# Block products on thirds (15 for 18) in place of halves (7 for 8) for the projections of a two-layer graph-attention kernel

## The chip, the cores and the metric

The kernel runs on one core of a Trainium2 chip. TensorE is the engine of the matrix products (matmuls); their results land in the banks of PSUM, from which ScalarE or VectorE read them (0.37 and 0.42 us for 128x256 in the trace of the kernel before). Tokens and weights lie in SBUF, the memory on the chip. GpSimd is a third engine for elementwise work, and transfers from and to the main memory (DMA) are issued by SyncE (SPq in the lines below). The time is the device time of one execution in microseconds (us); lower is better.

## The reference

128 graphs of 64 nodes with 768 features are normalised, sent through two attention layers and added to the input. All is fp32.

```python
h = jnp.maximum(_layernorm(x, axis=-1), 0.0)
for l in range(2):
    m_left  = einsum('bsh,oh->bso', h, W_left[l])
    m_right = einsum('bsh,oh->bso', h, W_right[l])
    u_left  = einsum('bih,bjh->bij', h, m_left) / temper        # u_right likewise
    u = u_left * adj_tri + u_left * diag_mask + u_right * swapaxes(adj_tri, 1, 2)
    delta_exp_u = exp(u) * adj
    attention = delta_exp_u / (sum(delta_exp_u, axis=2, keepdims=True) + 1e-10)
    h_lin = einsum('bsh,oh->bso', h, W_lin[l]) + b_lin[l]
    h = relu(layer_norm(attention @ h_lin, ln_a[l], ln_b[l]))
out = x + h
```

Nearly all the work is three 768x768 projections per layer: left, right and linear.

## The kernel before

Tokens go in 16 groups of 512. Each layer has a pass one (left and right projections, scores, softmax) and a pass two (linear projection, attention times it, layer norm). A projection is split in halves of inputs, outputs and tokens, and done as 7 block products instead of 8. The products run in PSUM banks X, Y, Z, V; a product that adds to an earlier one is chained in the same bank after it has been read.

```python
ORDER = (("X", "A11", "B11"), ("Y", "S2", "T2"), ("Z", "S1", "T1"), ("V", "S3", "T3"),
         ("X", "A12", "B21"), ("Z", "S4", "B22"), ("V", "A22", "T4"))

def project(u, k, g, between=None):            # once per side k and per 128 output columns g
    for i, (at, a, t) in enumerate(ORDER):
        ...                                    # a fresh bank at the first product in it
        for c in range(CH):                    # CH = 3
            nc.tensor.matmul(p, w[a][:, c, g * P:(g + 1) * P], b[t][:, c, :], ...)   # width 256
        ...                                    # one read of the bank per product (ScalarE or VectorE)
        pump(1)                                # one piece of side work from a queue
```

M, the projected tokens, lies in the long-lived pool `big`. The side work (normalising and transposing the next tokens, relu of loaded tokens, softmax steps, sums of tokens on GpSimd) comes from one queue, a piece per product.

Of the kernel before, what the change touches and what calls it, by code (L numbers as in the profile page):

```python
# [17 lines left out]
def kernel(  # L18
# [24 lines left out]

# [5 lines left out]
    CH = C // 2  # L49
    HH = H // 2  # L50
    PAIR = P // S
    Q = 4
# [3 lines left out]
    assert L == 2 and PAIR == 2 and C == 6 and HH <= 512  # L56
# [16 lines left out]
    queue = deque()  # L73
# [3 lines left out]
    def pump(n):  # L77
        for _ in range(n):
            f = queue.popleft() if queue else None
            if f is None and idle:  # L80
                f = idle.popleft()
            if f is not None:
                f()

    def flush():
        while queue:
            pump(1)


    SRC = {"l": w_left, "r": w_right, "n": w_lin}  # L90
    W = {}

    def load_w(l, kind):
        v = SRC[kind][l].rearrange("(c p) o -> p c o", p=P)
        t = {}
        for s in ("A11", "A21", "A22", "A12", "S1", "S2", "S4"):
            t[s] = wpool.tile([P, CH, HH], F32, name=f"w_{kind}_{s}")
        for s in ("A11", "A21", "A22", "A12"):
            i, o = int(s[2]) - 1, int(s[1]) - 1
            nc.sync.dma_start(t[s], v[:, i * CH:(i + 1) * CH, o * HH:(o + 1) * HH])  # L100
        W[l, kind] = t

    def centre(l):

        t = W[l, "n"]
        for a, b in (("A11", "A21"), ("A12", "A22")):
            m = stat.tile([P, 2, CH], F32, name="wm", bufs=2)
            idle.extend(none * 2)

            def means(a=a, b=b, m=m):  # L110
                nc.vector.reduce_sum(m[:, 0], t[a], axis=mybir.AxisListType.X)
                nc.vector.reduce_sum(m[:, 1], t[b], axis=mybir.AxisListType.X)
                nc.vector.tensor_add(m[:, 0], m[:, 0], m[:, 1])
                nc.vector.tensor_scalar_mul(m[:, 0], m[:, 0], 1.0 / H)

            idle.append(means)
            for s in (a, b):
                idle.extend(none * 2)
                idle.append(lambda s=s, m=m: nc.gpsimd.tensor_sub(
                    t[s], t[s], m[:, 0].unsqueeze(2).to_broadcast([P, CH, HH])))  # L120

    def sums_w(l, kind, eng, to, apart=0):
        t = W[l, kind]
        t["S3"] = t["A21"]
        for o, f, a, b in (("S1", "tensor_add", "S3", "A22"), ("S2", "tensor_sub", "S1", "A11"),
                           ("S3", "tensor_sub", "A11", "S3"), ("S4", "tensor_sub", "A12", "S2")):
            to.extend(none * apart)
            to.append(lambda o=o, f=f, a=a, b=b: getattr(eng, f)(t[o], t[a], t[b]))


    ORDER = (("X", "A11", "B11"), ("Y", "S2", "T2"), ("Z", "S1", "T1"), ("V", "S3", "T3"),
             ("X", "A12", "B21"), ("Z", "S4", "B22"), ("V", "A22", "T4"))
# [4 lines left out]
    def tokens_of(key):  # L137
        ht = HT[key]
        r = {f"B{i + 1}{t + 1}": ht[:, i * CH:(i + 1) * CH, t * TH:(t + 1) * TH]
             for i in range(2) for t in range(2)}  # L140
        r.update(TS.get(key, {}))
        return r

    def sums_t(key, eng=nc.gpsimd):

        ts = TS[key] = {}

        def sub(o, m, n):
            ts[o] = big.tile([P, CH, TH], F32, name="ts", bufs=6)
            b = tokens_of(key)  # L150
            eng.tensor_sub(b[o], b[m], b[n])  # L151

        for o, m, n in (("T1", "B12", "B11"), ("T2", "B22", "T1"), ("T3", "B22", "B12"), ("T4", "B21", "T2")):
            queue.append(lambda o=o, m=m, n=n: sub(o, m, n))
# [58 lines left out]
    def affine(which, l, u, step=1):  # L213
# [6 lines left out]
        for c in range(0, C if l else 0, step):  # L220
            queue.append(lambda c=c: part(c))

    def transpose_rows(l, u, pool):

        key, xr = (1, l, u), XR[l, u]
        if l == 0:
# [16 lines left out]
            if u:  # L243
                queue.extend(stats + [lambda: scale(0, Q)] + norms)
            else:
                scales = [lambda q=q: scale(q, q + 1) for q in range(Q)]
                queue.append(stats[0])
                for q in range(Q):
                    queue.extend(stats[q + 1:q + 2] + [scales[q], norms[q]])
        if (l, u) == (0, 0):  # L250
# [12 lines left out]
            for c in range(0, C, 2):  # L263
                queue.append(lambda c=c: turn(c))
            queue.append(lambda: nc.sync.dma_start(KEPT[l][u], ht))
            return
# [9 lines left out]
        for q in range(Q):  # L276
            queue.append(lambda q=q: nc.vector.transpose(
                xb[:, :, q, :], xr[q].rearrange("p (b j) -> p b j", j=32)))
        queue.append(store)


    def pass_one(l, aside):
        with tc.tile_pool(name=f"one{l}", bufs=2, reuse_waits="tile") as sp:
            ADJ, WM, CHAIN = {}, {}, {}
# [6 lines left out]
            def masks(u):  # L291

                WM[u] = sp.tile([P, Q, 2, S], F32, name="wm")
                for k in range(2):
                    t = tri[:, k].unsqueeze(1).to_broadcast([P, Q, S])
                    nc.gpsimd.tensor_tensor(WM[u][:, :, k], ADJ[u][:, :, 1 - k], t, op=ALU.mult)

            def softmax(u):
                return [lambda: next(CHAIN[u], None)] * 6

            def prepare(u):

                transpose_rows(l, u, sp)
                queue.append(lambda: load_h(1, l, u))
                if u + 1 < NB:
                    queue.append(lambda: load_rows(l, u + 1, sp))
                queue.extend(softmax(u - 2) if u > 1 else [])
                queue.append(lambda: load_adj(u))
                queue.extend(none * (6 if u > 1 else 9))
                affine(1, l, u)  # L310
                sums_t((1, l, u))

            M = {}

            def project(u, k, g, between=None):

                b, w = tokens_of((1, l, u)), W[l, "lr"[k]]
                bank = {}
                for i, (at, a, t) in enumerate(ORDER):
                    new = at not in bank  # L320
                    if new:
                        bank[at] = ps_st.tile([P, 512], F32, name=at)
                    p = bank[at][:, :TH]
                    for c in range(CH):
                        nc.tensor.matmul(p, w[a][:, c, g * P:(g + 1) * P], b[t][:, c, :],  # L325
                                         start=(new and c == 0), stop=(c == CH - 1),
                                         skip_group_check=True)
                    if i == 2 and k == 0 and g == 0:
                        M[u] = [big.tile([P, CH, T // S, 2, S], F32, name="n") for _ in range(2)]
                    if i >= 3:  # L330
                        half, first = ((1, 4), (0, 0), (0, 4), (1, 0))[i - 3]
                        to = M[u][half][:, g, first:first + 4, k, :]
                        pb = p.rearrange("p (b s) -> p b s", s=S)
                    if i == 0:
                        s1 = sp.tile([P, TH], F32, name="s1", bufs=1)
                        nc.scalar.copy(s1, p)  # L336
                    elif i == 1:
                        u2 = sp.tile([P, TH], F32, name="u2", bufs=1)
                        nc.vector.tensor_add(u2, p, s1)  # L339
                    elif i == 2:  # L340
                        u4 = sp.tile([P, TH], F32, name="u4", bufs=1)
                        nc.vector.tensor_add(u4, p, u2)  # L342
                    elif i == 4:
                        nc.scalar.copy(to, pb)  # L344
                    else:
                        nc.vector.tensor_add(to, pb, (u4 if i == 3 else u2).rearrange("p (b s) -> p b s", s=S))  # L346
                    if i == 1 and between:
                        between()
                    pump(1)

            def scores(u):

                ht, m = HT[1, l, u], M[u]
                p = ps_aux.tile([P, 2, T], F32, name="aux")[:, 0].rearrange("p (q m) -> p q m", q=Q)
                for q in range(Q):
                    for c in range(C):
                        for h in range(PAIR):
                            b = q * PAIR + h
                            nc.tensor.matmul(p[h * S:(h + 1) * S, q, :], ht[:, c, b * S:(b + 1) * S],  # L359
                                             m[c // CH][:, c % CH, b].rearrange("p k j -> p (k j)"),  # L360
                                             start=(c == 0), stop=(c == C - 1))
                wm, adj = WM[u], ADJ[u]

                def chain():
                    um = sp.tile([P, Q, 2, S], F32, name="um", bufs=1)
                    nc.vector.tensor_tensor(um.rearrange("p q k j -> p (q k j)"), p.rearrange("p q m -> p (q m)"),
                                            wm.rearrange("p q k j -> p (q k j)"), op=ALU.mult)
                    yield
                    v = sp.tile([P, Q, S], F32, name="v", bufs=1)
                    nc.vector.tensor_add(v, um[:, :, 0], um[:, :, 1])  # L370
# [12 lines left out]
                    at = sp.tile([P, 2, Q, 32], F32, name="at", bufs=1)  # L383
# [8 lines left out]

            if l == 0:
# [5 lines left out]
                transpose_rows(0, 0, sp)  # L399
# [289 lines left out]
```

## Time and profile before

| | before |
|---|---|
| time, median (lowest to highest of 4 runs) | 2944.11 us (2943.38 to 2945.45) |
| TensorE busy, instructions | 99%, 14872 |
| mean granted TensorE clock | 0.997 |
| VectorE, ScalarE, GpSimd busy | 38%, 20%, 26% |
| first product of the first group to first product of the second | 18.39 to 73.96 us = 55.57 us |

TensorE is the bound, and it stands for some 27 us in all: 12.5 us for ScalarE in the transposes at the very beginning, 11.8 us once in the middle, and about 2 us of small waits. The line of the 11.8 us is quoted in the prediction; that of the first is `PE aux L257 <- ACT x L239: 12.5, 4, 9.0` (us in total, times, longest). In the timeline the columns are start, duration, engine, source line, operation, output<-inputs, shapes, records; a bracket gives the idle time before and what ended it.

```profile
18.39 1.64 PE L325 MATMUL X<-ht,w_l_A 128*128 128x256 f32 x6
20.76 1.56 PE L325 MATMUL Y<-ts,w_l_S 128*128 128x256 f32 x6 [0.73 <-DVE ts L151]
```

The first product of this kernel uses raw weights and raw tokens, so it starts as soon as the tokens are transposed; only the second waits, 0.73 us, for a sum. A group of later tokens takes 59.98 us, of which 5.6 us are scores of the group before; without scores its own work is 54.4 us. The first group took 55.57 us. This kernel's start is nearly free of waits.

### The profile page before, as it was taken

To read this page: it belongs to the slowest core of one execution; us is meant where nothing else is said; L and a number is where in the kernel's file an instruction comes from. 1 tells how busy PE (TensorE), PEld (TensorE's weight loads), DVE (VectorE), ACT (ScalarE), POOL (GpSimd) and SP (SyncE) were. 2 spreads that over 40 slices of the span, in tenths; PEclk is the share of its full clock that TensorE was granted. 3 is DMA by queue.
4 is the path that set the end of the run, shared out by engine and by line. 5 is a ranking of instruction groups with operands and counts; after the bars stand their busy time and mean duration, and the time that the engine had idled before them with its cause. 6 is when DMAs were issued, how large, how long until landed. Compare 5 with 4: busy or idle time off the path is not lost.

```text
span 2942.2 us, 37469 instructions
## 1 busy us (share of the span) xinstructions
PE 2901.8 (99%) x14872; PEld 2241.3 (76%) x14872; DVE 1125.1 (38%) x2316; ACT 583.1 (20%) x1113; POOL 754.9 (26%) x478
## 2 busy tenths in 40 slices
PE   8999999999999999999998999999999999999998
PEld 7888888888888655555587888888888886555554
DVE  5444333433343232222333333333333324555555
ACT  2121112111120122222311111111111112232321
POOL 0321111111111262322312211111111114556564
PEclk9999999999999999999999999999999999999999
DMA  6424422342232343332454422343223304555544
GB/s 188 120 71 109 101 71 70 91 114 75 71 77 66 104 151 105 101 122 92 140 126 108 114 75 70 79 112 90 70 71 96 93 24 117 175 154 153 179 142 132
DMA packets 228656, 310.24 MB, mean 105 GB/s; under 512 B 53632, under 2 KB 179072, under 8 KB 220288
## 3 DMA queue, kind: packets, MB, share of 16 engines
q1 hardware_dynamic: 228192, 307.05, 37.6%
q8 instruction: 117, 1.92, 0.3%
q10 hardware_dynamic: 288, 0.79, 0.1%
q14 instruction: 59, 0.48, 0.1%
HBM read 202.91 MB, written 104.86 MB: 105 GB/s over the span
## 4 chain that ended last, share of the span: by engine, by line
PE 97%; DMA 1%; DVE 1%; SPq 0%; issue 0%; ACT 0%; POOL 0%; DVEq 0%; POOLq 0%
PE Z L325 17%; PE V L325 17%; PE X L325 17%; PE Y L325 8%; PE Z L567 8%; PE V L567 8%; PE X L567 8%; PE aux L359 6%; PE Y L567 5%; PE aux L495 3%; DMA x<-z 0%; DMA w_n_A<-in_w_lin_dram 0%; DMA h<-xb 0%; DMA at<-att 0%; PE aux L257 0%
## 5 line engine op out<-in xcount | busy, mean ns | idle before, releaser
L151 POOL TENSOR_TENSOR ts<-ht 128x768 f32<-128x768 f32 x126 | 241.0, 1913 | 1532.3 <-DMA ht<-h 579.5
L325 PE MATMUL V<-ts,w_l_A 128*128 128x256 f32 x1152 | 281.4, 380 | 11.8 <-DVE n L346 11.8
L325 PE MATMUL X<-ht,w_l_A 128*128 128x256 f32 x1152 | 280.2, 379 | 0.0
L325 PE MATMUL X<-ht,w_r_A 128*128 128x256 f32 x1152 | 280.2, 379 | 0.0
L325 PE MATMUL V<-ts,w_r_A 128*128 128x256 f32 x1152 | 280.0, 379 | 0.0
L567 PE MATMUL X<-w_n_A,ht 128*128 128x384 f32 x768 | 268.8, 486 | 0.0
L567 PE MATMUL V<-w_n_A,ts 128*128 128x384 f32 x768 | 268.6, 486 | 0.0
L344 ACT COPY n<-X 128x256 f32<-128x256 f32 x192 | 71.5, 372 | 968.8 <-PE X L325 968.8
L346 DVE TENSOR_TENSOR n<-V,u 128x256 f32<-128x256 f32 x384 | 161.9, 422 | 237.0 <-PE V L325 236.4
L325 PEld LDWEIGHTS V<-ts,w_l_A 128*128 128x128 f32 x1152 | 219.6, 191 | 42.1 <-DVE n L346 12.2
L151 POOL TENSOR_TENSOR ts<-ht,ts 128x768 f32<-128x768 f32 x126 | 238.8, 1895 | 40.6 <-issue 38.5
L325 PEld LDWEIGHTS X<-ht,w_l_A 128*128 128x128 f32 x1152 | 219.0, 190 | 30.3 <-issue 0.6
L325 PEld LDWEIGHTS X<-ht,w_r_A 128*128 128x128 f32 x1152 | 219.2, 190 | 29.9
L325 PEld LDWEIGHTS V<-ts,w_r_A 128*128 128x128 f32 x1152 | 218.9, 190 | 29.8
L567 PEld LDWEIGHTS V<-w_n_A,ts 128*128 128x128 f32 x768 | 145.9, 190 | 101.8
L567 PEld LDWEIGHTS X<-w_n_A,ht 128*128 128x128 f32 x768 | 145.8, 190 | 101.6 <-issue 0.3
L521 ACT ACTIVATE z<-aux 128x768 f32<-128x768 f32 x128 | 102.6, 807 | 596.5 <-PE aux L495 582.5
L339 DVE TENSOR_TENSOR u<-Y,s 128x256 f32<-128x256 f32 x192 | 81.5, 424 | 356.4 <-PE Y L325 349.4
L346 DVE TENSOR_TENSOR n<-Z,u 128x256 f32<-128x256 f32 x192 | 81.4, 424 | 304.2 <-PE Z L325 304.1
L342 DVE TENSOR_TENSOR u<-Z,u 128x256 f32<-128x256 f32 x192 | 81.5, 424 | 282.3 <-PE Z L325 282.1
L336 ACT COPY s<-X 128x256 f32<-128x256 f32 x192 | 71.2, 371 | 583.9 <-PE X L325 583.9
L577 POOL TENSOR_TENSOR u2b<-u,b 128x384 f32<-128x384 f32 x64 | 63.9, 999 | 474.1 <-DVE u L575 443.4
(107 smaller groups left out, 3959.4 us busy)
## 6 DMA issues: line engine op xcount, KB each, us to landing
ht<-h SPq DMA_DIRECT2D x63, 1536.0 KB, 7.0
h<-xb SPq DMA_DIRECT2D x124, 384.0 KB, 6.1
z<-z SPq DMA_DIRECT2D x128, 192.0 KB, 2.9
x<-z SPq DMA_DIRECT2D x128, 192.0 KB, 8.6
xr<-in_x_dram SPq DMA_DIRECT2D x128, 192.0 KB, 3.4
out_dram<-xr SPq DMA_DIRECT2D x128, 192.0 KB, 2.7
x<-in_x_dram SPq DMA_DIRECT2D x120, 192.0 KB, 8.3
adj<-in_adj_dram SPq DMA_DIRECT2D x64, 128.0 KB, 2.8
```

Of the source, the lines that this page charges most:

```text
L151: eng.tensor_sub(b[o], b[m], b[n])
L325: nc.tensor.matmul(p, w[a][:, c, g * P:(g + 1) * P], b[t][:, c, :], start=(new and c == 0), stop=(c == CH - 1), skip_group_check=True)
L336: nc.scalar.copy(s1, p)
L339: nc.vector.tensor_add(u2, p, s1)
L342: nc.vector.tensor_add(u4, p, u2)
L344: nc.scalar.copy(to, pb)
L346: nc.vector.tensor_add(to, pb, (u4 if i == 3 else u2).rearrange("p (b s) -> p b s", s=S))
L359: nc.tensor.matmul(p[h * S:(h + 1) * S, q, :], ht[:, c, b * S:(b + 1) * S], m[c // CH][:, c % CH, b].rearrange("p k j -> p (k j)"), start= ...
L495: nc.tensor.matmul(cx[k][i, m, :HH], at[j, q, :], hl[j, q, m * HH:(m + 1) * HH], start=True, stop=True)
L521: nc.scalar.activation(zs[k].rearrange(two, n=2), cx[k], AF.Square, accum_out=ss[:, k:k + 1])
L567: nc.tensor.matmul(p, b[t][:, c, r * P:(r + 1) * P], w[a][:, c, :], start=(new and c == 0), stop=(c == CH - 1), skip_group_check=True)
L577: nc.gpsimd.tensor_add(u2b, u2, rows["b2"])
```

## The change

The intent: fewer TensorE passes. Inputs and outputs are split in thirds of 256 features and tokens in halves: 18 block products, which a bilinear scheme does with 15. A block product is now 2 inner x 2 outer matmuls of width 256. In the linear projection that is 60 matmuls of width 256 per group instead of 42 of width 384, so fewer columns pass through TensorE although its instructions rise. All 15 are read from PSUM over 128x512, and banks are chained more tightly: X takes products 0, 2, 4, 6, 8, 10. In pass two the bias is copied into the fresh banks by ScalarE instead of being added afterwards. The queue gives way to numbered slots, two per product.

```diff
-    ORDER = (("X", "A11", "B11"), ("Y", "S2", "T2"), ...)                    # 7
+    ORDER = ((8, "X", "ta", "+2"), (5, "Z", "u1", "-0+2"), (0, "X", "u2", "+3"), (1, "Y", "u3", "-3"),
+             (12, "X", "B3", "-5"), (6, "V", "B0", "-2"), (2, "X", "td", "-4"), (4, "Y", "tb", "+1"),
+             (10, "X", "B4", "+0-2"), (7, "V", "B1", "+3"), (3, "X", "u0", "+1-3"), (11, "Y", "te", "+0"),
+             (13, "V", "tc", "-1"), (9, "Z", "tg", "+4"), (14, "V", "tf", "+5"))  # weight, bank, tokens, where it goes
+    W_SUMS = (...)   # 17 sums of 128x512 per weight matrix instead of 4 of 128x1152
+    T_SUMS = (...)   # 11 sums of 128x512 per group of tokens instead of 4 of 128x768

+    def read(p, to, i, seen):                 # first use of an output: ScalarE copies; later: VectorE adds
+        ...
+                nc.scalar.activation(to(o), p, AF.Copy, scale=1.0 if sign == "+" else -1.0)
+        ...
+                added(nc.vector, to(o), sign, to(o), p)

     def project(...):
-                    M[u] = [big.tile([P, CH, T // S, 2, S], F32, name="n") for _ in range(2)]
+                    M[u] = sp.tile([P, C, NBB, 2, S], F32, name="m", bufs=1)      # sp: the pool of this pass
...
     # start of layer 0
-                        sums_w(0, "r", nc.vector, queue, 1)
+                        rs = sums_w(0, "r", nc.gpsimd)
+                        for n in range(0, len(rs), 3):
+                            put(10 + n // 3, *rs[n:n + 3])
...
     def linear(...):                          # pass two, two blocks of 128 tokens together
+                    nc.scalar.copy(b, BIAS[:, PRELOAD[i]].unsqueeze(1).to_broadcast([P, len(rs), D]))
-                        nc.vector.tensor_add(s1, p, rows["b1"])
...
```

## The prediction

> **What bounds the kernel now.** I read the page from the top: busy shares, the slices, the chain that ended last, and then the groups with their shapes.

> ```profile
> span 2942.2 us, 37469 instructions
> PE 2901.8 (99%) x14872; PEld 2241.3 (76%) x14872; DVE 1125.1 (38%) x2316; ACT 583.1 (20%) x1113; POOL 754.9 (26%) x478
> ...
> PEclk9999999999999999999999999999999999999999
> ...
> PE 97%; DMA 1%; DVE 1%; SPq 0%; issue 0%; ACT 0%; POOL 0%; DVEq 0%; POOLq 0%
> ```

> The reader is to see that TensorE is the bound, at full clock, and that every other engine is below 40%. Only two things can move the time: fewer TensorE passes, or new TensorE idleness. So I need the pass time and the waits, from the timeline of TensorE.

> ```profile
> 434.97 1.46 PE L325 MATMUL X<-ht,w_l_A 128*128 128x256 f32 x6
> 436.26 1.46 PE L325 MATMUL Y<-ts,w_l_S 128*128 128x256 f32 x6
> 437.65 5.46 PE L359 MATMUL aux<-n,ht 128*64 128x128 f32 x96
> ...
> 1231.19 2.10 PE L567 MATMUL X<-w_n_A,ht 128*128 128x384 f32 x6
> 1233.13 2.10 PE L567 MATMUL Z<-w_n_S,ht 128*128 128x384 f32 x6
> ```

> A product is 3 matmuls and leaves 6 records, two per fp32 matmul. From start to start a product of width 256 takes 1.295 us, so 0.4317 us a matmul; one of width 384 takes 1.935 us, so 0.645 us. The mean of one record in the groups (380 ns, 486 ns) is longer than the step, because records overlap; it must not be multiplied by counts. The scores block takes 5.4 us and 0.2 us of change-over.

> The one long TensorE stall of this kernel is in the waits: V of L325 waited 11.8 us, once.

> ```profile
> PE V L325 <- DVE n L346: 11.8, 1, 11.8
> ...
> DVE wm L111 <- DMA w_n_A<-in_w_lin_dram: 11.6, 1, 11.6
> ```

> At 1552 us of the span VectorE stood in its queue at a sum over weights that had not landed, with a PSUM read behind it.

> [...] A record here is half an fp32 matmul, 215.8 ns from start to start[...]. [...] the trace has 681 ns for the 128x512 product with a PSUM operand (L366). [...] the trace has 1283 ns in all 31 of them.

> **The change part by part.**

> 1. *Projections of the tokens (left, right).* Before: 2 sides x 3 output columns x 7 products x 3 matmuls = 126 matmuls of width 256 per group of 512 tokens. After: 2 x 15 products x 2 x 2 = 120, same width and weight shape. There are 16 groups x 2 layers: 192 matmuls fewer x 0.4317 = **-83 us**. "15 for 18" sounds like a sixth, but the old form already had 7 for 8, so it is 1/21.

> 2. *The linear projection.* Before: 42 matmuls of width 384 per group, 27.09 us. After: 60 of width 256, 25.90 us. Difference 1.19 x 32 = **-38 us**. More weight loads, but the left/right stage already runs loads at this rate with TensorE at its step.

> 3. *Reads of PSUM.* They get twice as wide: 18 reads of 128x512 per 15 products, 6 on ScalarE (590 ns, the copy from PSUM at L260) and 12 on VectorE (681 ns). Per project 8.2 us of VectorE in 25.9 us: throughput is no question. Latency is. Bank X is used at products 0, 2, 4, 6, 8, 10 with a single product between. A product lasts 4 x 0.4317 = 1.727 us; the record of the last matmul ends 0.16 us after its step, VectorE starts 0.04 us later (in the timeline), TensorE restarts 0.05 us after a read. Left for the reads: 1.727 - 0.25 = 1.47 us. One read on ScalarE fits. Product 8 has two VectorE reads: 2 x 0.681 + 0.04 = 1.40 us plus some 0.1 us for a weight load that can't be taken ahead: zero to 0.13 us of wait, in 64 projects and 32 linears. I take 0.07 x 96 = **+7 us**.

> 4. *What stands ahead of those reads.* This I followed in the order of instructions of the changed kernel. In layer 0, ahead of the read of product 4 on ScalarE, stand the table load (1.28), the square root (0.3, then 0.4 for VectorE's reciprocal and bias) and three normalisations of 128x768 (1.02 each, L239). Count from the end of product 0: scores to 5.5, product 1 to 7.2, product 2 to 8.95, its read to 9.75, table and root to 11.3, first normalisation from 11.75, third done at 14.6, read of product 4 done at 15.2. Product 6 could start at 14.1: about 1.1 us of wait. At product 14 the softmax on VectorE (with a table load for Exp) delays the read of product 12 by some 0.3 us. Together 1.4 x 15 groups = **+20 us**. In layer 1 there are no normalisations, and the softmax lies before product 8: nothing.

> 5. *Start, borders, end.* The first sums of weights and tokens (31 instead of 8 for the left side) run on VectorE ahead of products 0 to 14: start 2.3 us later and some 4 us of waits: **+6 us**. At the border from pass one to pass two, product 0 now needs a bias preload on ScalarE, queued behind the last softmax's Exp, some 3.5 us after the scores; before, TensorE went straight on: 2 x 3.5 = **+7 us**. The last group of each linear stage runs in products of half the size (0.86 us) with only 0.6 us for reads: **+6 us** for two. Its last context waits for the previous one's buffers: 2 x 3 = **+6 us**.

> 6. *The stall of 11.8 us.* The sums over weights now come some 12 free slots later, after the weights have landed: **-12 us**.

> 7. *GpSimd.* 11 token sums of 128x512 (1.3 us, estimated from 1.9 us for 128x768) instead of 4: 14 us per group instead of 7.6, in 57 or 29 us. They are done well before product 6 of the next group: off the path. The bias adds of pass two on GpSimd go.

> Sum: -83 - 38 - 12 + 7 + 20 + 6 + 7 + 6 + 6 = -81. 2944.6 - 81 = **2864 us**, 2.7% faster.

> **The rivals.**

> *The bare count of passes.* If the reads always hide, only 1, 2 and 6 remain with a few us at the borders: about 2820 us. For it: the wider reads are below half the throughput of both engines. Against: with one product between two uses of X, and in-order queues, any normalisation or softmax step ahead of a read becomes TensorE idleness, which the old order (X again after 4 products, 5.2 us) could absorb.

> *The banks become the bound.* If the two-read gap at product 8 costs 0.4 us rather than 0.07 (a read slowed by the strided output, or VectorE late), that is 96 x 0.33 = 32 us more: 2896 us, within 2%. For it: my slack there is zero. Against: the strided reads of 128x256 took 422 ns now[...], and even beside a busy GpSimd they don't spread. VectorE's steps with two SBUF inputs do: the last add of pass two (L534) takes 1.41 us on the mean, 0.95 us alone.

> *The last pass overloads VectorE or the transfers.* There VectorE has 12 reads, 4 scaled products (1.0 us) and 4 last adds (up to 1.7 us), about 19 of 29 us per group, and TensorE's slots must wait for ScalarE's relu of tokens still being loaded (7 us per load, 155 GB/s in this stage). One or two us per group would add 15 to 30 us: 2880 to 2895 us. Against: I followed the queue and found read 12 done at 5.05 us where product 14 starts at 5.18.

> **Range and chances.** The gains (133 us) rest on counts and a step measured to a per mille; I trust them to 3 us. The losses (52 us) are sums of small waits that could be 20 or 110. Hence 2836 to 2894. Faster by over 2% means below 2885.7 us: losses below 74 us. I give that 0.80; within 2% 0.19; slower would need 190 us of waits, against which the other engines' shares speak: 0.01.

> **What would show it right or wrong.** The step of width 256 should still be 1.295 us per 6 records, with 7680 records in the left/right stage and 3840 in the linear. A group of the left/right stage should take 57.4 us in layer 1 and about 58.8 in layer 0 (60.0 now); a pair of linears 29.2 to 29.4 us (30.4 now). Waits of TensorE for ScalarE should stand at X in layer 0, those for VectorE at X after product 8 with under 0.15 us each. The 11.8 us wait should be gone. Wrong would be: GpSimd named as TensorE's releaser, waits at X in layer 1, or a linear pair over 30 us.

What is left of the cut paragraph are times measured in the kernel before; its last clause means ScalarE's 31 table loads of 1283 ns. That a product chained into a bank waits for the read of the one before, on which steps 3 and 4 rest, is seen there in V's wait of 11.8 us: the product starts at 1565.25 us, 0.05 us after VectorE's read of V (0.42 us from 1564.78 us). The 0.1 us for a weight load in step 3 is the difference between 1.56 us for a product whose first load starts with it (at 443.04 us) and 1.46 us for one whose load starts 0.21 us earlier (at 436.26 us). The strided reads of 128x256 that "don't spread" take 0.43 us at most, alone as beside GpSimd; the last add of pass two takes 0.95 us in all 29 cases alone and up to 2.54 us beside it.

## The result and the profile after

The output is correct. The changed kernel took 2898.03 us (median of 4 runs, 2894.96 to 2902.79) against 2944.11: the ratio is 0.9844, 95% interval 0.9827 to 0.9861. Ratios here are the mean time of one kernel's runs over that of the other's runs of the same rounds, so not quite the ratio of the medians. The gain is 1.6%, where 2.7% was predicted, and 2898.03 lies 4 us above the predicted range.

The head of the page of the changed kernel, with its slices of granted clock and its chain of what ended last:

```profile
span 2896.5 us, 39904 instructions
PE 2804.7 (97%) x15640; PEld 2387.1 (82%) x15640; DVE 1307.7 (45%) x2126; ACT 842.5 (29%) x1453; POOL 1195.0 (41%) x934
...
PEclk8999999999999999999999999999999999999998
...
PE 83%; DMA 6%; DVE 4%; ACT 4%; SPq 1%; issue 1%; POOL 0%; ACTq 0%; DVEq 0%; POOLq 0%
```

TensorE's share fell from 99% to 97% and its part in the chain from 97% to 83%: more of that chain is now work of others that TensorE waits for. The first and the last slice of the clock are at 8 tenths; the mean clock is 0.989, where it was 0.997. The waits of TensorE in the changed kernel (engine, bank, line, what it waited for: us in total, times, longest):

```profile
PE X L354 <- ACT m L189: 31.8, 22, 7.3
PE aux L293 <- ACT x L275: 12.3, 4, 8.9
PE X L601 <- ACT hl L189: 8.2, 3, 5.5
PE X L354 <- DVE w_l L144: 7.8, 2, 5.7
PE Y L354 <- DVE w_l L144: 5.4, 1, 5.4
PE X L601 <- ACT X L584: 4.8, 2, 2.4
```

The 11.8 us stall is gone, and the 12.3 us of the beginning stand in both kernels. The rest is new. The steady state is what the prediction said. Second group of layer 0, the timeline of TensorE:

```profile
105.12 1.89 PE L354 MATMUL X<-ht,w_l 128*128 128x256 f32 x8
106.85 1.89 PE L354 MATMUL V<-ht,w_l 128*128 128x256 f32 x8
109.80 1.97 PE L354 MATMUL X<-ts,w_l 128*128 128x256 f32 x8 [1.06 <-ACT m L189]
```

A product starts 1.73 us after the one before, 4 x 0.432 us as before the change. Product 6, in X, waits 1.06 us for ScalarE's read of product 4, in 14 groups: the wait of step 4, at the place named there. From scores to scores a group of layer 0 takes 58.68 us (59.98 before), the best groups of layer 1 57.39 us, and a pair of linears 29.20 us. The excess is elsewhere, in places that come once or twice each.

**The beginning.** Timeline of the changed kernel, GpSimd, VectorE and TensorE:

```profile
14.73 27.25 POOL L144 TENSOR_TENSOR w_r<-w_r,w_r 128x512 f32<-128x512 f32 x17 [12.98 <-DMA w_r<-in_w_right_dram]
...
19.04 5.08 DVE L144 TENSOR_TENSOR w_l<-w_l,w_l 128x512 f32<-128x512 f32 x3
...
24.18 3.78 PE L354 MATMUL X<-ts,w_l 128*128 128x256 f32 x8 [5.71 <-DVE w_l L144]
...
37.42 0.67 DVE L144 TENSOR_TENSOR m<-m,Z 128x512 f32<-128x512 f32 x1
37.56 3.78 PE L354 MATMUL Y<-ts,w_l 128*128 128x256 f32 x8 [5.36 <-DVE w_l L144]
...
49.25 2.74 DVE L144 TENSOR_TENSOR w_l<-w_l,w_l 128x512 f32<-128x512 f32 x4
```

Three left-weight sums take VectorE 5.08 us while GpSimd sums the right weights, some 1.67 us each from start to start; four take 2.74 us once GpSimd has finished at 42.0 us, 0.60 us from start to start, or 0.72 us where a sum reads the result of the one before. The add at 37.42, which has one operand in PSUM, takes its usual 0.67 us even beside GpSimd. The products that follow these waits of 5.71 and 5.36 us last 3.78 us instead of 1.89. The second group starts at 92.63 us instead of 73.96. Less each kernel's own work (51.8 us and 54.4 us), that is 40.8 us against 19.6: the beginning costs 21 us more.

**The first group of layer 1.** Timeline of the changed kernel:

```profile
1464.79 0.60 ACT L189 ACTIVATE m<-X 128x512 f32<-128x512 f32 x1 [4.40 <-DMA z<-z]
...
1465.53 3.75 PE L354 MATMUL X<-ts,w_l 128*128 128x256 f32 x8 [7.32 <-ACT m L189]
```

ScalarE's first read of X waits for a store of `z`, rows of the pass before. M has moved from `big` into the pool of the pass, whose memory those rows still held. In the same group:

```profile
1495.15 0.34 SPq L248 DMA_DIRECT2D ht<-h  x1
...
1502.10 1.52 ACT L255 ACTIVATE ht<-ht,b_col,a_col 128x512 f32<-128x512 f32 x2 [7.67 <-DMA ht<-h]
1503.52 0.57 ACT L189 ACTIVATE m<-X 128x512 f32<-128x512 f32 x1
...
1504.15 3.57 PE L354 MATMUL X<-ht,w_r 128*128 128x256 f32 x8 [6.91 <-ACT m L189]
```

Here ScalarE stands at the relu of tokens whose load has been issued at 1495.15, and the read of X is behind it in its queue. X is named with `m` and ScalarE, but the true releaser is the transfer, which landed at 1502. The product starts 0.06 us after the read ends (1503.52 + 0.57). Further groups of layer 1 show the same wait with 0.2 to 1.25 us. Their mean over 14 groups is 57.74 us, 0.35 us over the best; in the control run below it is only 0.10 us over it, so this part differs from run to run. In the first linear of layer 1 it comes a third time, 5.47 us before the product at 2419.60.

**The borders.** The two waits of 2.4 us for the bias copy in X (L584), where pass one turns into pass two.

### The profile page after: what moved, and what is told of

Its sections match the earlier page's. It is cut to its first block, busy times and chain, and to the rows that moved or that the text cites. A ratio compares the mean times of both kernels' runs of the same rounds, so it can differ in the third digit from the quotient of the medians.

```text
span 2896.5 us, 39904 instructions
## 1 busy us (share of the span) xinstructions
PE 2804.7 (97%) x15640; PEld 2387.1 (82%) x15640; DVE 1307.7 (45%) x2126; ACT 842.5 (29%) x1453; POOL 1195.0 (41%) x934
## 4 chain that ended last, share of the span: by engine, by line
PE 83%; DMA 6%; DVE 4%; ACT 4%; SPq 1%; issue 1%; POOL 0%; ACTq 0%; DVEq 0%; POOLq 0%
PE X L354 18%; PE V L354 12%; PE X L601 11%; PE Y L354 9%; PE V L601 8%; PE Z L354 6%; PE aux L376 6%; PE Y L601 5%; PE Z L601 4%; PE aux L520 3%; DMA ht<-h 2%; DMA h<-xb 2%; ACT ht L255 1%; DVE st L220 1%; ACT x L275 1%
## 5 line engine op out<-in xcount | busy, mean ns | idle before, releaser
L144 POOL TENSOR_TENSOR ts<-ht 128x512 f32<-128x512 f32 x441 | 585.8, 1337 | 1227.2 <-DMA ht<-h 519.5
L144 POOL TENSOR_TENSOR ts<-ht,ts 128x512 f32<-128x512 f32 x189 | 249.3, 1324 | 200.7 <-PE X L354 99.6
L354 PE MATMUL X<-ts,w_l 128*128 128x256 f32 x1024 | 246.8, 384 | 27.8 <-ACT m L189 22.1
L601 PE MATMUL X<-w_n,ts 128*128 128x256 f32 x1024 | 246.0, 382 | 6.6 <-ACT X L584 4.8
L354 PE MATMUL X<-ts,w_r 128*128 128x256 f32 x1024 | 242.9, 380 | 2.9 <-ACT m L189 2.8
L354 PEld LDWEIGHTS X<-ts,w_l 128*128 128x128 f32 x1024 | 193.0, 192 | 63.1 <-issue 28.3
L601 PEld LDWEIGHTS X<-w_n,ts 128*128 128x128 f32 x1024 | 193.0, 191 | 38.4 <-issue 5.8
L354 PEld LDWEIGHTS X<-ts,w_r 128*128 128x128 f32 x1024 | 191.4, 190 | 34.9 <-ACT m L189 6.1
L354 PE MATMUL Y<-ts,w_l 128*128 128x256 f32 x768 | 183.7, 382 | 5.4 <-DVE w_l L144 5.4
L601 PE MATMUL Y<-w_n,ts 128*128 128x256 f32 x768 | 182.4, 379 | 0.0
L354 PE MATMUL Y<-ts,w_r 128*128 128x256 f32 x768 | 181.4, 379 | 0.0
L354 PEld LDWEIGHTS Y<-ts,w_l 128*128 128x128 f32 x768 | 147.4, 192 | 26.2 <-DVE w_l L144 5.8
L354 PEld LDWEIGHTS Y<-ts,w_r 128*128 128x128 f32 x768 | 145.9, 190 | 19.8
```

The lines of the kernel that those rows point to most:

```text
L144: (eng.tensor_add if sign == "+" else eng.tensor_sub)(o, a, b)
L354: nc.tensor.matmul(p[:, g], w[ORDER[i][0]][:, c, g * P:(g + 1) * P], b()[t][:, c, :], start=(new and g == c == 0), stop=(c == K2 - 1), ski ...
L601: nc.tensor.matmul(p[:, n], b[t][:, c, r * P:(r + 1) * P], w[s][:, c, :], start=(i in FIRST and i not in PRELOAD and n == c == 0), stop=(c ...
```

## The experiments

The control and e1 to e3 ran on one chip together, e4 to e7 on another, each with 9 runs of the kernel before (median 2942.56 and 2943.4 us). A gain over the control is given as the difference of the two ratios times 2943 us; since each ratio has an interval of about 0.0013 to either side, such a gain is known to some 5 us, and where it is smaller the trace has to decide.

**c_after**, the changed kernel, unaltered, as control.

> The changed kernel again, unaltered, on the chip and in the rounds of the three that follow: a control. All theories: 2898 us within 0.2%, ratio to before 0.984 to 0.986. In the profile the first product of the second group (X at the left side) starts at 92 to 93 us, layer 0 has 14 waits of 1.06 us at X, and layer 1 begins with waits of some 7 us each at X.

Measured: 2895.49 us, ratio 0.9839 (0.9826 to 0.9853), clock 0.990. The result stands. Its trace has a little less waiting in layer 1 (the row X L354 <- ACT m: 29.6 us in 18 waits).

**e1_gate.** GpSimd's sums of the right weights are held until VectorE has finished the left ones, by a copy of one column.

```diff
-                        for n in range(0, len(rs), 3):
-                            put(10 + n // 3, *rs[n:n + 3])
+                        held = stat.tile([P, 1], F32, name="held", bufs=1)
+                        put(14, lambda: nc.gpsimd.tensor_copy(held, W[0, "l"][7][:, 0, 0:1]))
+                        for n in range(0, len(rs), 3):
+                            put(14 + n // 3, *rs[n:n + 3])
```

> GpSimd's 17 sums for the right-hand weights wait for the last of VectorE's sums for the left-hand weights; nothing else differs. Theory A (the two engines slow each other on steps with two SBUF inputs): VectorE's sums of 128x512 before product 4 fall from 1.67 us start to start to about 0.60, the second group starts at 78 to 82 us rather than 92.6, and the time falls by 11 to 15 us. Theory B (VectorE waits for weights that land late): the sums stay where they are and the time doesn't fall. If the right-hand sums come too late, TensorE waits for GpSimd at the start of the right-hand side (about 48 us), and some of the gain is lost.

Measured: 2885.72 us, ratio 0.9807 (0.9794 to 0.9821), 9.4 us under the control where 11 to 15 were expected, so lower, but within the error of some 5 us. The second group starts at 81.64 instead of 92.63 us, 11.0 us sooner, as expected. The timeline of this run:

```profile
27.00 3.46 DVE L144 TENSOR_TENSOR w_l<-w_l,w_l 128x512 f32<-128x512 f32 x5
...
30.01 1.97 PE L354 MATMUL X<-ht,w_l 128*128 128x256 f32 x8 [0.83 <-DVE w_l L144]
...
37.38 23.21 POOL L144 TENSOR_TENSOR w_r<-w_r,w_r 128x512 f32<-128x512 f32 x17
...
40.19 1.58 DVE L144 TENSOR_TENSOR ts<-ht,ts 128x512 f32<-128x512 f32 x1
...
50.20 3.78 PE L354 MATMUL Z<-ts,w_l 128*128 128x256 f32 x8 [1.82 <-DVE ts L144]
```

The same left-weight sums now step at 0.60 to 0.73 us, and product 4 starts at 30.01 instead of 43.40 us. So it is GpSimd's company that slowed them, not the sums themselves. The operands matter: 0.60 to 0.73 us in this trace against 1.67 us in that of the changed kernel for the sums of two SBUF operands, 0.67 us in either case for the adds with a PSUM operand. What the two engines share is not shown. It costs both, VectorE most: in the changed kernel GpSimd's sums step at 1.60 us beside VectorE's (27.25 us for 17), while a sum of tokens takes it 1.27 us at 1510 us; so the common step of 1.67 us is below the sum of the two single ones, 1.87 us. Some of the gain is given back, because VectorE's last token sums now meet GpSimd's (1.58 us at 40.19), and TensorE waits 1.94 us at 46.00 and 1.82 us at 50.20: from product 11 to the right side it takes 13.57 us, 9.65 before the edit. TensorE's waits for reads of X later on are longer in this trace, too (35.5 us, 29.6 in the control); whether the edit did that is not shown.

**e2_norms.** In layer 0, one of the four normalisations goes before the read of product 4, two after it and the last after the read of product 6; VectorE's transposes of these rows follow them.

```diff
-                todo.extend(stats + [lambda: scale(0, Q)] + norms)
+                todo.extend(stats + [lambda: scale(0, Q)])
...
+            todo.extend([norms[0], None, turns[0], norms[1], norms[2], turns[1], turns[2], norms[3], turns[3]])
```

> Layer 0: one normalisation ahead of ScalarE's read of product 4, two behind it, the fourth behind the read of product 6, the transposes likewise. Theory A (the wait at product 6 is ScalarE's in-order queue): the 14 waits of 1.06 us at X go, the group takes 57.5 us rather than 58.7, and the time falls by 14 to 17 us. Theory B (the wait is the latency of a ScalarE read as such, or of the chained bank): product 6 waits as before, no change in time.

Measured: 2880.14 us, ratio 0.9788 (0.9774 to 0.9801), 15.0 us under the control. Timeline of this run, products 5 and 6 of the second group:

```profile
107.83 1.89 PE L357 MATMUL V<-ht,w_l 128*128 128x256 f32 x8
109.55 1.89 PE L357 MATMUL X<-ts,w_l 128*128 128x256 f32 x8
```

The wait of 1.06 us is gone in every group. From scores to scores the 14 groups take 57.39 us (three) or 57.75 us (eleven) instead of 58.68 to 59.18, in sum 15.0 us less than in the control, which is what was gained. ScalarE's queue order, not its load, cost it.

**e3_big.** M and the linear's output go back into pool `big`, as before the change.

```diff
-                        M[u] = sp.tile([P, C, NBB, 2, S], F32, name="m", bufs=1)
+                        M[u] = [big.tile([P, C, NBB // 2, 2, S], F32, name="n") for _ in range(2)]
...
-                    HL[u] = sp.tile([P, Q, H], F32, name="hl", bufs=2)
+                    HL[u] = big.tile([P, Q, H], F32, name="n")
```

> The left/right products and the linear results share buffers that outlive the passes again, as in the kernel before, rather than buffers of each pass. Theory A (the 7.3 us wait at the start of layer 1 is memory of pass one that pass two's last rows still occupied until their transfers landed): that wait shrinks to below 1.5 us, the slow product behind it (3.4 us rather than 1.7) goes too, and the time falls by 7 to 10 us. Theory B (ScalarE is late because of its own work on the last rows of layer 0): the wait stays at 4 us or more and the time falls by less than 4 us.

Measured: 2887.72 us, ratio 0.9818 (0.9804 to 0.9831), 6.2 us under the control (7 to 10 expected). The timeline at the start of layer 1:

```profile
1460.07 0.60 ACT L189 ACTIVATE n<-X 128x512 f32<-128x512 f32 x1
...
1460.81 1.97 PE L354 MATMUL X<-ts,w_l 128*128 128x256 f32 x8 [2.85 <-ACT n L189]
```

The read no longer waits for the store of `z`; 2.85 us remain, where theory A said under 1.5, for ScalarE's squares and scales of the last rows, which stand ahead of it in the queue. The product after the wait is at full speed. So the memory of the pool was the larger part of the wait.

**e4_relu.** The relu of the next tokens in layer 1 moves behind the landing of their load, and GpSimd's sums of these tokens move with it.

```diff
-                return todo + affine(1, l, u)
+                return todo
...
+                if l and u + 1 < NB:
+                    put_all(45, affine(*nxt))
+                    put_sums_t(nxt, 51, 0, 30)
...
+                    if last and not u:
+                        put_all(15, affine(2, l, u + 1))
+                        put_sums_t((2, l, u + 1), 21, 0, 0)
...
```

> Layer 1: ScalarE's relu of the next group's tokens is put behind the read of product 7, the last read of a PSUM bank that ScalarE makes in a project, in all groups of pass one and in the first of pass two. Theory A (ScalarE stands in its queue at a relu whose transfer has not landed, with a PSUM read behind it): the waits of 6.9 us (second side of the first group), 1.25 and 0.2 to 0.4 us (later groups) and 5.5 us (pass two) go, with two slow products of 1.7 us: 15 to 19 us less. Theory B (the chained banks make TensorE wait at X in layer 1 anyway): waits at X of the same sum stay. If GpSimd's sums then come too late, TensorE will be seen waiting for GpSimd.

Measured: 2873.23 us, ratio 0.9763 (0.9749 to 0.9776), 22.4 us under the control, where 15 to 19 were expected. The waits of TensorE in this run:

```profile
PE X L354 <- ACT m L189: 22.2, 15, 7.3
...
PE X L605 <- ACT hl L189: 2.8, 2, 1.7
```

What is left in the first row are the 14 waits of layer 0 and the 7.3 us of layer 1's start. Against the control's trace the two rows fell by 7.4 and 5.4 us, and the slow products of layer 1 cost about 5.3 us less, 18 us in all, inside the expected range. In this profile slow products at the start, the border and the end cost some 5 us less, too, where the edit changes nothing: that part of the gain is luck. (What slow products cost is an estimate: half of TensorE's busy time in the stretches in which `--windows` shows a granted clock of 0.50.)

**e5_pre.** The bias of the first product of pass two is copied into X ahead of the last scores instead of behind the softmax.

```diff
...
+            bank = ps_st.tile([P, 2 * TH], F32, name="X").rearrange("p (r d) -> p r d", r=2)
+            nc.scalar.copy(bank, rows["bias", l][:, 0].unsqueeze(1).to_broadcast([P, 2, D]))
+            READY.append(bank)
             scores(NB - 1)
...
```

> At the border from pass one to pass two the bias is copied into bank X ahead of the last scores, not behind the last Exp. Theory A: the two waits of 2.4 us for ScalarE's copy go, and the slow products behind them: 5 to 8 us less. Theory B (TensorE would wait for the tokens or for the softmax's banks there): the waits get another name and the time stays within 2 us.

Measured: 2892.61 us, ratio 0.9829 (0.9815 to 0.9842): 2.9 us under the control, too little to tell apart by the time. The timeline of this run tells why:

```profile
981.24 1.99 PE L604 MATMUL X<-w_n,ts 128*128 128x256 f32 x8 [1.13 <-ACT hl L189]
...
2413.84 3.71 PE L604 MATMUL X<-w_n,ht 128*128 128x256 f32 x8 [9.21 <-ACT hl L189]
```

Both waits of 2.4 us are gone, but at the first border 1.13 us come back one product later, behind the Exp, and at the second the wait for the loaded tokens grew from 5.47 to 9.21 us: TensorE arrived earlier at a transfer that was no earlier. What the edit gains once e4's edit has removed that wait was not run with these two alone; in e6, which has both, neither wait is left at the second border.

**e7_warm.** To tell a slow product from a slow read: 14 needless matmuls into a spare bank fill the wait at the start of layer 1. Nothing else is altered; one look, no timing.

```diff
+                    if l == 1 and u == k == 0 and i == 1:
+                        spare = ps_st.tile([P, 2 * TH], F32, name="Y")
+                        for n in range(14):
+                            nc.tensor.matmul(spare[:, :TH], w[8][:, 0, :P], b()["ta"][:, 0, :], ...)
```

> The changed kernel with 14 needless matmuls of width 256 into a free bank inside the 7.3 us wait at the start of layer 1. Theory A (the product after the wait is slow because TensorE's clock was lowered while it stood idle): the product after the wait takes 1.73 to 1.9 us rather than 3.4 to 3.75, and the granted clock around it reads 1.0. Theory B (it is slow because of the wait itself, e.g. weights loaded late): it stays at 3.4 us or more. The total hardly moves (2 us).

The timeline of this run:

```profile
1456.62 6.21 PE L367 MATMUL Y<-ts,w_l 128*128 128x256 f32 x28
1464.11 1.97 PE L354 MATMUL X<-ts,w_l 128*128 128x256 f32 x8 [1.28 <-ACT m L189]
```

The wait for the read ends where it did (1464.11 us; 1463.98 in the control), but the product behind it takes 1.97 us, not 3.54 as in the control or 3.75 as in the first run. The windows of 7 us around it (busy time and instructions of TensorE, its weight loads, VectorE, ScalarE and GpSimd; then granted clock, DMA share, GB/s), first of the changed kernel, then of this run:

```profile
1463.00:1470.00 7.00, 4.47 (x11) 3.62 (x12) 0.69 (x1) 1.68 (x3) 0.00 (x0) 0.51 0.97 239
```

```profile
1463.00:1470.00 7.00, 5.89 (x27) 5.24 (x28) 1.38 (x2) 2.12 (x4) 0.00 (x0) 1.00 0.99 235
```

The granted clock is 0.51 in the window with the idle time and 1.00 where TensorE was kept busy. So this wait is paid for twice: once as 7.3 us of idle time, once as a product at half clock. The same goes for the five waits of 5.4 to 7.3 us in the trace of the changed kernel, with products of 3.57 to 3.78 us behind them. Shorter waits can do it as well. In the changed kernel one of 2.38 us (before the product at 980.38 us) was enough, with 2.45 and 3.13 us for the two products behind it. In e1 two waits, of 1.94 and 1.82 us, followed each other closely, with this in the windows:

```profile
44.01:47.42 3.41, 1.47 (x8) 1.29 (x8) 3.03 (x6) 0.30 (x1) 3.33 (x4) 1.00 0.00 0
47.42:50.84 3.42, 1.60 (x5) 0.79 (x4) 3.37 (x7) 2.48 (x3) 3.26 (x3) 0.50 0.00 0
```

**e6_all.** The five edits together.

> All five edits together. If each wait was independent, the gains add: 12 + 15 + 9 + 17 + 7 = 60 us, so 2838 us, range 2830 to 2850, 3.6% faster than the kernel before. If removing one wait lets another take its place (transfers that start earlier collide, GpSimd's queue becomes the releaser), the sum falls short: above 2855 us.

Measured: 2837.36 us (2835.97 to 2838.75), ratio 0.964 (0.9627 to 0.9653), 58.6 us under the control and 3.6% faster than the kernel before. Correct, the fastest of all, and inside the expected 2830 to 2850. The single gains add up to 9.4 + 15.0 + 6.2 + 22.4 + 2.9 = 55.9 us. So no loss from the edits together is seen; but the error of the control enters that sum several times, and a difference under some 18 us (an estimate from the intervals) could not be told. The page of this run:

```profile
span 2836.7 us, 39921 instructions
PE 2790.6 (98%) x15640; PEld 2382.0 (84%) x15640; DVE 1301.9 (46%) x2126; ACT 843.9 (30%) x1453; POOL 1189.6 (42%) x935
```

The number of TensorE instructions is that of the changed kernel, 15640, and the mean clock is back at 0.997.

## Why the prediction was wrong

The prediction was 2864 us, 2836 to 2894; the kernel took 2898. The gains of 133 us came; the losses were 86 us (2898 - 2944.6 + 133) instead of 52. The prediction said of them that they "could be 20 or 110", but its range ends at 82, so the range was narrower than its own doubt. By its own steps:

1. *Projections of the tokens* and 2. *The linear projection*: right. The step is 1.727 us a product, a group's work and a pair of linears (29.20 us) are as predicted.
3. *Reads of PSUM*: predicted +7 us, measured none. Two reads by VectorE at product 8 take 1.28 us together, not 1.40, because the second starts 0.60 us after the first: in a row, these reads counted with their step and not with their duration. The rival in which the banks become the bound fell with it.
4. *What stands ahead of those reads*: right for layer 0: 58.68 us a group where 58.8 was predicted, with the wait at product 6 as worked out; e2 shows that the normalisations ahead of that read caused it. Wrong for layer 1. "In layer 1 there are no normalisations, and the softmax lies before product 8: nothing" left out the two things that stand in ScalarE's queue there: the relu of loaded tokens, which waits for a transfer, and the first read into M, which waits for memory that stores of the pass before still use. They cost 8.6 + 4.9 us and 9.5 us with the slow products behind them; of the last, 2.85 us of waiting are ScalarE's own work on the last rows, as e3 shows. I had put "waits at X in layer 1" down as a sign of being wrong, and so it was. The third rival had named relu on loaded tokens, but for the last pass and in every group; it came there once, 8.5 us with its two slow products.
5. *Start, borders, end*: the start is the term that was mis-sized most: +6 predicted, +21 measured. (It counts 31 first sums; the kernel has 28, 17 of weights and 11 of tokens.) I gave VectorE's sums their ordinary duration beside a GpSimd that reads SBUF the whole time, although my second rival had just noted that "VectorE's steps with two SBUF inputs do" spread beside it. e1 shows this part, 11.0 of the 15 us too few; the half clock is in both numbers. The borders cost about 8 us (7 predicted); the half-size products of the linear ends 2.7 us (6 predicted), the last contexts 3.7 us (6 predicted).
6. *The stall of 11.8 us*: right, gone. The trace of the kernel before showed the slow product behind it, too, 2.93 us instead of 1.46, and the prediction passed over it:

```profile
1565.25 2.93 PE L325 MATMUL V<-ts,w_l_A 128*128 128x256 f32 x6 [11.76 <-DVE n L346]
```

7. *GpSimd*: its token sums stay off the path, but its weight sums at the beginning did not; it is not named in TensorE's waits, since it acted through VectorE.

The missing cost: 15 (start) + 9.5 + 8.6 + 4.9 + 8.5 + 1 (borders) = 47.5 us. The overestimated: 7 + 3.3 + 2.3 = 12.6 us. The difference, 34.9 us, agrees with the miss of 34 us to 1 us. The failed steps are therefore step 5's "start" and step 4's "In layer 1 ... nothing". A cause that occurs in no step of mine, the half clock behind idle time, is part of these terms: in the profile of the changed kernel TensorE is busy for 34 us in stretches with a granted clock of 0.50, so some 17 us are lost, against 1.6 us in the kernel before (an estimate, as in e4). It differs from run to run: 16 us in the control, the same kernel. `--windows` shows the half clock at each of these places; that keeping TensorE busy prevents it, e7 shows at one.

## What to carry to other kernels

Fewer passes pay most of what the count says (106 of 133 us in e6) as long as the queues of the reading engines hold nothing that waits: put each piece of side work that depends on a transfer behind its landing (e4: 22.4 us under the control), and each run of side work in pieces smaller than the slack between two uses of a bank (e2: 15.0 us). When a sum moves to GpSimd, look for what VectorE reads from SBUF in that time (1.67 us a sum instead of 0.60 at the start of the changed kernel). A wait of TensorE of several us should be charged with the slower product behind it as well (3.57 to 3.78 us instead of 1.89 behind the waits of 5.4 to 7.3 us), and so should short waits that follow each other within some 3 us (3.78 us behind those of 1.94 and 1.82 us in e1).
